# Turning V's weights with VectorE instead of TensorE in a conditioned attention kernel

## The chip, the cores and the metric

The kernel runs on one core of one Trainium2 chip. The metric is the device time of one execution in microseconds. Before the change the median of three runs is 736.79 us (736.71 to 736.79). A core has five engines that run their own instruction streams side by side: TensorE (PE in the profile, its weight loads PEld), VectorE (DVE), ScalarE (ACT), GpSimd (POOL) and SyncE (SP), which here only issues DMA transfers. They wait for each other through semaphores.

## What is computed

The reference is one attention layer over x (8 batches, 512 positions, 512 channels, float32) with a token per batch that conditions queries and keys, and a residual:

```
Q = split_heads(x @ Wq.T + bq);  K, V likewise      # 16 heads of 32
tQ = split_heads(tokens @ Wq.T + bq);  tK likewise  # one token per batch
cQ = Q + tQ;  cK = K + tK
attn = softmax(cQ @ cK.T / sqrt(32))
out  = x + merge_heads(attn @ V)
```

## The kernel before

The work is cut into 32 groups: 8 batches times 4 groups of four heads (128 channels). Channels of a group lie on the 128 partitions. All weight matrices must be turned, because the product contracts over the input channel, so `wT["q"]`, `wT["k"]` and `wT["v"]` hold W transposed: partition = input channel within a block of 128, then four such blocks, then 512 output channels.

The order of the instructions on TensorE, VectorE, ScalarE and GpSimd is written out by hand (`manual_schedule`): each engine takes its instructions in the order of the program text. SP is left to the planner, which places its DMA issues by when their buffers come free. PSUM is one tile of eight banks of 512 floats; `bank(i)` names one, and the table `TURNS` names the banks of each stage by place.

**The head of the program**, up to about 28 us, is where the change lies. The first loads are x's first batch, then the weights in rows of 2 KB: `load_w` (L175 to L178), one DMA of 256 KB per 128 rows, so that partition p of block c holds row c·128+p of W. Behind them on SP's queue stand bvb and bvs (copies of the bias of V) and then, by `load_block`, the blocks of x's second batch, in runs of 128 bytes: `spread` (L135) views a 512x512 matrix so that row f·32+j goes to partition j, place f, and takes 32 columns. Such a block, turned by VectorE in squares of 32x32 (`turn_x`, L310), is x transposed, without TensorE. `load_residual` (L159, L169) loads and biases the x that is added at the end, and writes it out in the same spread layout.

`transpose_w` (L249) turns 128 rows of a weight matrix with four TensorE transposes (L253) into one PSUM bank, from which VectorE (L260, L264) or ScalarE (L262, L266) copies it to `wT`. `project_qk_part` (L337) is one of the four products, one per block of input channels, of a group's queries or keys in the plain form; `project_qk_end` adds the token's part on the way out of PSUM: VectorE for q (L350), ScalarE for k (L352). The first two groups' q and k come from this plain form. All later projections use a form with seven products in place of eight (`first_products`, `other_products`, L390 and L393), whose sums of weight blocks GpSimd makes once (`combine_w`, L282 to L285) from `wT`, into the buffers of the raw weights.

The token's part of q or k is `condition` (L644: four products of the tokens with wT, one per quarter of TensorE's columns, then a ScalarE copy L646) and `condition_end`: four TensorE transposes of that copy (L631), a reduction by VectorE (L653) and an addition of the bias (L659; VectorE for q, GpSimd for k).

In the text the last steps of the head run like this: the last eight of k's weight transposes, w_v's first four, `condition_end("q")`, `condition("k")`, w_v's next four, `condition_end("k")`, w_v's last eight, with q's and k's group 0 finished between, and then all of q's second group in bank 7. After that come `combine_w` and the first row of scores: `row_max(0, 0)` (L486 on TensorE, four score tiles; L477 and L495 on VectorE, their row maxima), `denominators` (L505 on ScalarE, the exponentials with their sums), the second group's k (L337, finished by ScalarE's L352), the second row of scores, and the first seven-product stage for q (L393).

**The body** goes over the groups t, four stages each; a stage holds 4 tiles of exponentials (L547 and L550 on TensorE, L561 on ScalarE), one row of scores of the next group with its maxima and sums, and either one stage of a projection for the next batch or the products of the group before with V (L566). `split_max` (L519 to L522, GpSimd) cuts the row maxima into three bfloat16 parts, which TensorE transposes (L531) and adds to the scores. GpSimd takes its work in program order too, so a biasing of a residual (L169) can stand ahead of a split_max.

Of the kernel before, what the change touches and what calls it, by code (L numbers as in the profile page):

```python
# [17 lines left out]
def kernel(  # L18
# [38 lines left out]
    nc = tc.nc  # L57
    P = 128
# [4 lines left out]
    HG = P // HD  # L63
    NP = HG // 2
    NS = S // P
    NC = D // P
# [65 lines left out]
    BL = 32  # L132
    NB = S // BL

    def spread(a, d):  # L135

        return a.rearrange("(f j) d -> j f d", j=BL)[:, :, d : d + BL]
# [33 lines left out]
    ws = {}  # L171
# [3 lines left out]
    def load_w(n, w, queue, cs=range(NC)):  # L175
        wv = w.rearrange("(c p) d -> p c d", p=P)
        for c in cs:
            queue.dma_start(ws[n][:, c, :], wv[:, c, :])  # L178
# [29 lines left out]
    load_w("k", Wk, nc.sync, [0])  # L208
    load_w("q", Wq, nc.sync, [1, 2, 3])
    load_w("k", Wk, nc.sync, [1, 2, 3])  # L210
    load_w("v", Wv, nc.sync)
    bvb = const.tile([P, D], F32, tag="bvb", name="bvb")
    nc.sync.dma_start(bvb, bv.rearrange("(o d) -> o d", o=1).broadcast_to([P, D]))
    bvs = const.tile([P, G, BL], F32, tag="bvs", name="bvs")
# [18 lines left out]
    for i in range(NS):  # L233
# [11 lines left out]
    wT = {  # L245
        n: const.tile([P, NC, D], F32, tag=f"wT{n}", name=f"wT_{n}") for n in ("q", "k", "v")
    }

    def transpose_w(n, dc, pt, odd=None):  # L249

        odd = dc % 2 if odd is None else odd
        for cc in range(NC):
            nc.tensor.transpose(  # L253
                pt[:, cc * P : (cc + 1) * P], ws[n][:, dc, cc * P : (cc + 1) * P], ident
            )
        o = wT[n][:, :, dc * P : (dc + 1) * P]
        pv = pt.rearrange("p (c s) -> p c s", c=NC)
        if n == "q":
            if odd:
                nc.vector.tensor_scalar(o, pv, SCALE, None, ALU.mult)  # L260
            else:
                nc.scalar.activation(o, pv, AF.Copy, scale=SCALE)  # L262
        elif odd:
            nc.vector.tensor_copy(o, pv)  # L264
        else:
            nc.scalar.copy(o, pv)  # L266
# [62 lines left out]
    def pair_of(t, n):  # L329

        if (n, t // 2) not in pairs:
            pairs[n, t // 2] = qkp.tile([P, 2, S], F32, tag=n, name=f"{n}T_{t // 2}")
        return pairs[n, t // 2]

    def project_qk_part(t, n, cc, pt):
        b, g = divmod(t, G)
        nc.tensor.matmul(  # L337
            pt,
            wT[n][:, cc, g * P : (g + 1) * P],
            xT[b][:, cc, :],  # L340
            start=(cc == 0),
            stop=(cc == NC - 1),
        )

    def project_qk_end(t, n, pt):
        b, g = divmod(t, G)
        o = pair_of(t, n)[:, t % 2, :]
        add = tok[:, "qk".index(n), g, b : b + 1]
        if n == "q":
            nc.vector.tensor_scalar(o, pt, add, None, ALU.add)  # L350
        else:
            nc.scalar.activation(o, pt, AF.Identity, bias=add)  # L352
        qkT[n, t] = o

    def project_qk(t, n, pt):
        for cc in range(NC):
            project_qk_part(t, n, cc, pt)
        project_qk_end(t, n, pt)
# [281 lines left out]
    def condition(n, pt):  # L640


        for cc in range(NC):
            nc.tensor.matmul(pt[cc * HD : (cc + 1) * HD, :], condT[:, cc, :], wT[n][:, cc, :])  # L644
        part[n] = const.tile([P, D], F32, tag=f"part{n}", name=f"part_{n}")
        nc.scalar.copy(part[n], pt)  # L646

    def condition_end(n, pt, on):

        i = "qk".index(n)  # L650
        untranspose(part[n], pt)
        sum4 = const.tile([P, NC, B], F32, tag=f"sum4{n}", name=f"sum4_{n}")
        nc.vector.tensor_reduce(  # L653
            sum4,
            pt.rearrange("p (d c e) -> p d e c", d=NC, c=NC)[:, :, 0:B, :],
            AX.X,
            ALU.add,
        )
        on.tensor_tensor(  # L659
            tok[:, i], sum4, bias2[:, i, :].unsqueeze(2).broadcast_to([P, NC, B]), ALU.add  # L660
        )
# [5 lines left out]
    def bank(i):  # L667
        return psum[:, i, :]
# [27 lines left out]
    condition("q", bank(6))  # L696
    transpose_w("k", 2, bank(3), 1)
    transpose_w("k", 3, bank(7), 0)
    transpose_w("v", 0, bank(0), 1)
    condition_end("q", bank(1), nc.vector)  # L700
    project_qk_end(0, "q", pq)
    condition("k", bank(5))
    transpose_w("v", 1, bank(6), 1)
    condition_end("k", bank(0), nc.gpsimd)
    transpose_w("v", 2, bank(3), 0)
    project_qk_end(0, "k", pk)
    transpose_w("v", 3, bank(1), 1)
    project_qk(1, "q", bank(7))
    for n in ("q", "k", "v"):
        combine_w(n)  # L710

# [266 lines left out]
```

## Time and profile before

| what | value |
|---|---|
| median of three runs | 736.79 us |
| the profiled execution: its time | 736.38 us |
| its span, first to last instruction | 734.3 us |
| mean granted TensorE clock in it | 0.999 of full speed |
| TensorE busy | 726.8 us, 99% of the span |
| ScalarE busy | 618.9 us, 84% |
| VectorE busy | 530.0 us, 72% |
| GpSimd busy | 182.8 us, 25% |
| w_v's four DMA issues on SP | from 8.3 to 9.7 us, each landed 4.8 to 5.5 us later |
| w_v's sixteen transposes on TensorE | 19.4 to 23.4 us |

The difference of 2.1 us between the profiled execution's time and its span is what lies before the first and after the last instruction. In the rows of the profile, the first number is the start in us from the beginning of the span, the second the duration; a merged row with "x8" gives the duration of all eight. A float32 product shows as two passes, so four products read x8 in the L337 and L644 rows, while transposes read one each. In brackets stands how long the engine had been idle and what ended that.

### The profile page before, as it was taken

The numbers are of one execution on the slowest core, as the hardware profiler recorded it, in microseconds if no ns is written. First come the engines' busy times: TensorE is split into PE (matmuls) and PEld (weight loads), VectorE is DVE, ScalarE is ACT, GpSimd is POOL, SyncE is SP. The second block draws the span as 40 slices with busy tenths as digits, with TensorE's granted clock in tenths as the row PEclk, the third lists the DMA queues.
The fourth block names the chain that finished last, engine by engine and source line by source line (L and its number), as shares of the span: only waits on it lengthen the run. The fifth ranks groups of instructions, "written<-read, shape, count | busy, mean of one in ns | idle before, by whom it ended". The sixth has DMA issues, their size and how long they took to land.

```text
span 734.3 us, 15120 instructions
## 1 busy us (share of the span) xinstructions
PE 726.8 (99%) x5432; PEld 405.7 (55%) x5432; DVE 530.0 (72%) x844; ACT 618.9 (84%) x1543; POOL 182.8 (25%) x282
## 2 busy tenths in 40 slices
PE   9999999999999999999999999999999999999997
PEld 6566555665555565555565555565555566555422
DVE  3688776776777876777776877777767777767665
ACT  2478988988988988988989888988988899898665
POOL 3720211222211122221122221122221122221363
PEclk9999999999999999999999999999999999999999
DMA  8521212222212212211212221212110111110112
GB/s 260 88 45 29 45 23 36 40 34 45 44 28 32 44 30 44 45 31 29 44 30 44 44 34 25 44 30 44 29 24 10 28 30 29 30 27 10 24 16 43
DMA packets 194270, 29.63 MB, mean 40 GB/s; under 512 B 190986, under 2 KB 192010, under 8 KB 194196
## 3 DMA queue, kind: packets, MB, share of 16 engines
q1 hardware_dynamic: 193616, 28.01, 22.9%
q8 instruction: 42, 0.69, 0.4%
q10 hardware_dynamic: 580, 0.68, 0.3%
q14 instruction: 32, 0.26, 0.1%
HBM read 20.27 MB, written 8.39 MB: 39 GB/s over the span
## 4 chain that ended last, share of the span: by engine, by line
PE 97%; ACT 1%; DVE 1%; DMA 1%; issue 0%; POOL 0%; DVEq 0%; POOLq 0%
PE psum L393 26%; PE psum L566 16%; PE psum L486 15%; PE psum L550 15%; PE psum L390 14%; PE psum L547 6%; PE psum L337 2%; PE psum L531 1%; PE psum L253 1%; ACT e L561 1%; DMA x<-in_x_dram 1%; PE psum L576 0%; PE psum L298 0%; DVE nmax L495 0%; PE psum L644 0%; PE psum L631 0%
## 5 line engine op out<-in xcount | busy, mean ns | idle before, releaser
L505 ACT ACTIVATE dead<-psum,nmax 128x512 f32<-128x512 f32 x480 | 327.0, 701 | 7.8 <-DVE nmax L477 5.4
L561 ACT ACTIVATE e<-psum 128x512 f32<-128x512 f32 x512 | 264.4, 603 | 77.9 <-PE psum L550 77.8
L477 DVE TENSOR_REDUCE nmax<-psum 128x1 f32<-128x512 f32 x240 | 154.6, 686 | 144.4 <-PE psum L486 144.4
L495 DVE TENSOR_REDUCE nmax<-psum 128x2 f32<-128x1024 f32 x136 | 164.7, 1216 | 10.4 <-PE psum L486 9.1
L623 POOL TENSOR_TENSOR res<-res,recs 128x512 f32<-128x512 f32 x31 | 33.3, 1076 | 446.8 <-DVE res L622 446.8
L486 PE MATMUL psum<-kT,qT 32*128 32x512 f32 x1024 | 136.3, 601 | 0.0
L550 PE MATMUL psum<-qT,kT 32*128 32x512 f32 x1024 | 133.0, 589 | 0.0
L566 PE MATMUL psum<-e,v 128*32 128x512 f32 x1024 | 120.5, 597 | 0.0
L505 ACT ACTIVATION_READ_ACCUMULATOR dead<-psum,nmax 128x1 f32 x480 | 104.9, 218 | 0.0
L486 PEld LDWEIGHTS psum<-kT,qT 32*128 32x128 f32 x1024 | 57.7, 183 | 56.6 <-ACT dead L505 19.7
L566 PEld LDWEIGHTS psum<-e,v 128*32 128x32 f32 x1024 | 26.3, 110 | 65.2 <-issue 37.7
L547 PE MATMUL psum<-maxT,onesb 3*128 3x512 bf16 x512 | 52.6, 385 | 0.0
L550 PEld LDWEIGHTS psum<-qT,kT 32*128 32x128 f32 x1024 | 51.1, 186 | 2.4 <-issue 0.2
L390 PE MATMUL psum<-wc_v,xc 128*128 128x256 f32 x192 | 49.5, 380 | 0.4 <-ACT e L561 0.4
L547 PEld LDWEIGHTS <-onesb 3*128 3x128 bf16 x512 | 13.5, 91 | 61.5 <-issue 51.8
L393 PE MATMUL psum<-xc,wc_q 128*128 128x256 f32 x180 | 46.2, 379 | 0.0
L393 PE MATMUL psum<-xc,wc_k 128*128 128x256 f32 x180 | 46.2, 379 | 0.0
L624 POOL TENSOR_TENSOR res<-res,xr 128x512 f32<-128x512 f32 x31 | 40.4, 1302 | 2.4
L169 POOL TENSOR_TENSOR xr<-xr,bvs 128x512 f32<-128x512 f32 x31 | 39.3, 1268 | 3.2 <-DMA xr<-in_x_dram 2.9
L390 PEld LDWEIGHTS psum<-wc_v,xc 128*128 128x128 f32 x192 | 36.4, 190 | 6.1 <-ACT e L561 1.3
L390 PE MATMUL psum<-wT_v,xT 128*128 128x256 f32 x128 | 38.8, 405 | 0.0
L393 PEld LDWEIGHTS psum<-xc,wc_q 128*128 128x128 f32 x180 | 34.3, 190 | 4.6
(156 smaller groups left out, 778.5 us busy)
## 6 DMA issues: line engine op xcount, KB each, us to landing
xr<-in_x_dram SPq DMA_DIRECT2D x124, 64.0 KB, 2.5
out_dram<-res SPq DMA_DIRECT2D x124, 64.0 KB, 2.0
x<-in_x_dram SPq DMA_DIRECT2D x112, 64.0 KB, 2.3
w_q<-in_L_cond_Wq_dram SPq DMA_DIRECT2D x4, 256.0 KB, 4.5
w_k<-in_L_cond_Wk_dram SPq DMA_DIRECT2D x4, 256.0 KB, 4.3
w_v<-in_L_cond_Wv_dram SPq DMA_DIRECT2D x4, 256.0 KB, 5.2
x<-in_x_dram ACTq DMA_DIRECT2D x2, 256.0 KB, 4.4
x<-in_x_dram SPq DMA_DIRECT2D x2, 256.0 KB
```

What stands on the lines that cost most here:

```text
L169: nc.gpsimd.tensor_tensor(xr[t], xr[t], bias, ALU.add)
L390: nc.tensor.matmul(pt, xb, w, start=(kc == kcs[0]), stop=(kc == kcs[-1]))
L393: nc.tensor.matmul(pt, w, xb, start=(kc == kcs[0]), stop=(kc == kcs[-1]))
L477: nc.vector.tensor_reduce(nmax[t][:, qc, j : j + 1, 0], banks(HG + j), AX.X, ALU.max, negate=True)
L486: nc.tensor.matmul(pt, qkT["q", t][r, qc * P : (qc + 1) * P], qkT["k", t][r, :], start=True, stop=True,)
L495: nc.vector.tensor_reduce(nmax[t][:, qc, pr * 2 : pr * 2 + 2, 0], pt, AX.X, ALU.max, negate=True)
L505: nc.scalar.activation(dead, banks(HG + j), AF.Exp, bias=nmax[t][:, qc, j, :], accum_out=sums[t][:, qc, j, :],)
L547: nc.tensor.matmul(bank[j], onesb[r, :], maxT[t][r, :], start=True, stop=False)
L550: nc.tensor.matmul(bank[j], qkT["k", t][r, kc * P : (kc + 1) * P], qkT["q", t][r, :], start=False, stop=True,)
L561: nc.scalar.activation(e[:, i, :], bank[pr * 2 + i], AF.Exp)
L566: nc.tensor.matmul(pt[j * HD : (j + 1) * HD, :], vs[b % 2][:, kc, (g * HG + j) * HD : (g * HG + j + 1) * HD], es[t, kc, j // 2][:, j % 2, ...
L624: nc.gpsimd.tensor_tensor(y, y, xr.pop(t), ALU.add)
```

## The change

V's weights are loaded in sixteen DMAs of 64 KB instead of four of 256 KB, in runs of 128 bytes (32 floats) instead of 2 KB, in the layout that `spread` makes: partition h·32+j of block cc holds, for f from 0 to 15, the 32 columns from cc·128+h·32 of row f·32+j. The four calls of `transpose_w("v", ...)` go: sixteen transposes on TensorE, three copies on VectorE, one on ScalarE. Four VectorE transposes of 128x512 take their place, after `project_qk_end(0, "k")` in the text, which on VectorE puts them behind the reduction of `condition_end("k")` and ahead of the end of q's second group. Two of the four products of q's second group (bank 7) move up between `condition("k")` and `condition_end("k")`; the other two stay after it.

```
-    load_w("v", Wv, nc.sync)
+    wv = ws["v"].rearrange("p c (f e) -> p c f e", e=BL)
+    for cc in range(NC):
+        for h in range(HG):
+            nc.sync.dma_start(
+                wv[h * BL : (h + 1) * BL, cc], spread(Wv, cc * P + h * BL)
+            )
...
     transpose_w("k", 3, bank(7), 0)
-    transpose_w("v", 0, bank(0), 1)
     condition_end("q", bank(1), nc.vector)
     project_qk_end(0, "q", pq)
     condition("k", bank(5))
-    transpose_w("v", 1, bank(6), 1)
+    for cc in range(2):
+        project_qk_part(1, "q", cc, bank(7))
     condition_end("k", bank(0), nc.gpsimd)
-    transpose_w("v", 2, bank(3), 0)
     project_qk_end(0, "k", pk)
-    transpose_w("v", 3, bank(1), 1)
-    project_qk(1, "q", bank(7))
+    for cc in range(NC):
+        nc.vector.transpose(wT["v"][:, cc, :], ws["v"][:, cc, :])
+    for cc in range(2, NC):
+        project_qk_part(1, "q", cc, bank(7))
+    project_qk_end(1, "q", bank(7))
```

In the built program SP's order changes too: the blocks x_8 and x_9 of the third batch's x are issued ahead of the residual load xr_0, x_10 ahead of xr_1, x_11 ahead of xr_2; before, xr_0, xr_1 and xr_2 went first.

## The prediction

> **What bounds the kernel now.** I read the page's busy shares first, then the chain that ended last.
>
> ```profile
> PE 726.8 (99%) x5432; PEld 405.7 (55%) x5432; DVE 530.0 (72%) x844; ACT 618.9 (84%) x1543; POOL 182.8 (25%) x282
> PE 97%; ACT 1%; DVE 1%; DMA 1%; issue 0%; POOL 0%; DVEq 0%; POOLq 0%
> ```
>
> TensorE is busy 99% of the span and carries 97% of the chain. So work taken from TensorE shortens the run, as long as nothing else is late where the gap closes. The change lies between 8 and 60 us, so I read the timeline there.
>
> ```profile
> 18.47 1.09 PE L253 MATMUL psum<-ident,w_k 128*128 128x128 f32 x8
> ...
> 19.40 0.60 PE L253 MATMUL psum<-ident,w_v 128*128 128x128 f32 x4
> ...
> 19.61 0.59 ACT L266 COPY wT_k<-psum 128x512 f32<-128x512 f32 x1 [0.41 <-PE psum L253]
> ...
> 20.37 0.16 PEld L644 LDWEIGHTS psum<-wT_k,condT 128*32 128x32 f32 x8 [0.17 <-ACT wT_k L266]
> 20.37 1.06 PE L644 MATMUL psum<-wT_k,condT 128*32 128x512 f32 x8
> ...
> 21.37 0.66 PE L253 MATMUL psum<-ident,w_v 128*128 128x128 f32 x4
> 21.50 0.58 ACT L646 COPY part_k<-psum 128x512 f32<-128x512 f32 x1 [1.31 <-PE psum L644]
> ...
> 22.14 0.66 PE L631 MATMUL psum<-ident,part_k 128*128 128x128 f32 x4
> 22.64 1.04 PE L253 MATMUL psum<-ident,w_v 128*128 128x128 f32 x8
> 22.84 0.29 DVE L653 TENSOR_REDUCE sum_k<-psum 128x32 f32<-128x128 f32 x1
> ...
> 23.51 3.60 PE L337 MATMUL psum<-xT,wT_q 128*128 128x512 f32 x8
> ```
>
> A row is start, duration, engine, line. The w_v rows go away; the L337 row is q's second group, of which half moves up. Next, what follows:
>
> ```profile
> 27.22 0.75 DVE L350 TENSOR_SCALAR qT<-psum,tok 128x512 f32<-128x512 f32 x1 [2.82 <-PE psum L337]
> 28.20 1.29 DVE L477 TENSOR_REDUCE nmax<-psum 128x1 f32<-128x512 f32 x2 [0.23 <-PE psum L486]
> 28.92 0.69 ACT L505 ACTIVATE dead<-psum,nmax 128x512 f32<-128x512 f32 x1 [4.48 <-DVE nmax L477]
> 31.74 1.14 PE L486 MATMUL psum<-kT,qT 32*128 32x512 f32 x8
> 32.05 0.69 ACT L352 ACTIVATE kT<-psum,tok 128x512 f32<-128x512 f32 x1
> 32.81 0.92 PE L393 MATMUL psum<-xT,wT_q 128*128 128x256 f32 x3
> ```
>
> This chain decides the forecast. ScalarE's second kT (L352) ends at 32.05+0.69 = 32.74 and TensorE's L393 starts at 32.81. It must wait: its first product goes to bank 4, which that kT reads (both take place 1 of their row of TURNS, 4 in each). The list of waits agrees:
>
> ```profile
> PEld psum L393 <- ACT kT L352: 0.8, 1, 0.8
> ```
>
> So VectorE and ScalarE have next to no slack at 32.8, though neither is the bound of the kernel.
>
> **TensorE alone.** Sixteen transposes go. The first four (19.40 to 19.84) are worth nothing: the token's product for k starts at 20.37, released by ScalarE's copy of wT_k that ends at 20.20, and that copy waits for k's own transposes, which don't move. Without w_v, TensorE idles there. The next four end a stretch of 22.14-21.37 = 0.77, of which 0.44 is work and the rest the wait for part_k (ready at 22.08). The last eight are 23.51-22.64 = 0.87. Together 1.64.
> In their place, q's first half starts at 21.37 plus 0.06 (eight transposes behind L644 took 0.93, elsewhere 0.87), lasts four passes of 0.43 = 1.72, and ends at 23.15, so part_k is no longer waited for. Its four transposes take 0.43, to 23.58; the second half, with the 0.09 that L337 spends in front of L486 (27.04-23.51 is 3.53, eight passes are 3.44), ends at 25.40. Before, L486 started at 27.04: 1.64 earlier.
>
> **kT of group 0, now later against TensorE.** part_k's transposes start at 23.15 (before: 22.14). VectorE's sum_k follows 0.64 to 0.70 later (23.08 to 23.71 for the last w_v copy, 22.14 to 22.84 here): 23.79 to 23.85, end at most 24.14. GpSimd's tok: 0.08 of wait and 0.24. ScalarE then starts 0.05 to 0.30 later (no row shows it waiting for GpSimd; before, its kT stood at 23.75 behind another copy, 0.30 after tok ended at 23.45), and takes 0.69: 25.1 to 25.45. Against 25.40 that is at most 0.1 of wait, covered by what comes next.
>
> **VectorE: three copies go, four transposes of w_v come, and where they stand is the price.** Program order puts them between sum_k and q's second L350. VectorE is idle from 22.0 (the end of q's first L350) to sum_k, so an earlier place would be free; this one isn't. Nearest row: the transpose of x, the same 128x512 f32 from SBUF to SBUF.
>
> ```profile
> 45.17 0.70 DVE L310 STREAM_TRANSPOSE xT<-x 128x512 f32<-128x512 f32 x1
> 45.26 2.50 POOL L169 TENSOR_TENSOR xr<-xr,bvs 128x512 f32<-128x512 f32 x2
> ```
>
> Two in a row take 1.29 and the second starts 0.62 after the first. From sum_k (23.82) it goes: 0.25 to the first transpose, 4 x 0.62 = 2.48, L350 0.67 start to start: L477 starts at 27.22. By TensorE it could have started at 25.40+1.16 = 26.56 (28.20-27.04 = 1.16). Before it was 28.20, so this chain gains 0.98, not 1.64. ScalarE follows L477 step for step, so its second kT ends at 32.74-0.98 = 31.76, and L393 starts at about 31.83, while TensorE would be there at 31.17. It idles for about 0.65 and keeps a gain of 0.98. Bounds by the spread of these steps (pace 0.60 to 0.65, first step 0.23 to 0.32, sum_k 23.79 to 23.85): 0.8 to 1.1. If the chain had slack I don't see, 1.64.
> GpSimd's wc_q runs beside the transposes. Row first: above, a transpose beside a GpSimd operation takes 0.70, the four of x 0.67 to 0.70, and the two GpSimd operations 1.25 each, their usual time. The Trainium skill, SBUF — State Buffer, § Summary: rules for kernel authors, says that when VectorE runs in a two-port mode the one of the two that issues second blocks fully until the other ends. By it each transpose could wait for one 1.26 us operation, 5 us in all and a slower kernel; by the row, nothing. I take the row.
> Behind L393 the order repeats every 4.29 us with TensorE back to back, so all else shifts along.
>
> **w_v's loads.** 4 issues of 256 KB become 16 of 64 KB in 128-byte runs, on SP's queue ahead of bvb, bvs and x's blocks. Nearest row:
>
> ```profile
> 14.14 9.69 SPq L145 DMA_DIRECT2D x<-in_x_dram  x16
> ```
>
> That is 0.61 per issue; the xr ones take 6.32/12 = 0.53. From 8.26, sixteen are issued by 16.7 to 18.0 and landed 2.5 later, 20.5 at the latest. By bytes: 1.05 MB at the 109 to 133 GB/s of 18 to 30 us, behind 3.15 MB of x, w_q and w_k (moved by about 11.0, adding up GB/s by stretch), is 7.9 to 9.6: at most 20.6[...]. VectorE wants them at 24.07: hidden.
> The rule against this: DMA: Bandwidth & Descriptors, § Measured, gives 0.95 us for 64 KB and calls smaller transfers descriptor-dominated. Sixteen in series are 15.2 (estimate): 26.2, some 28 landed, and about 3.8 us on VectorE's chain: 739.6. By the rows, 735.8. I take the rows: same runs, same queue.
> SP's queue behind it is some 7.5 us later: x_4 goes out at about 21.6, the fourth block lands at 34, wanted at 43.5. The build also puts the residual loads xr_0 and xr_1 behind the blocks x_8 and x_9, x_10, which wait for VectorE's transposes at 50 and 56 us. xr_1 then lands at about 61 (before: by 33), and GpSimd's addition to it stands in front of split_max of group 1 (65.11 before, about 64 now), whose result TensorE uses at 70.12 before, 69 now. 1.27+1.23 after 61 is 63.5: hidden, with 5 us to spare.
>
> **The sum.** The profiled execution has a span of 734.3 and a time of 736.38; minus 0.98 that is 733.3 and 735.4. The median of the runs is 736.79, 0.41 above: 735.8.
>
> **Rivals.** I call a change within 0.2% (1.47 us) the same: that is about what a measurement of this kernel can tell from no change.
> Full gain: ScalarE's kT isn't what holds L393, and all of 1.64 stays: 735.15. For it: no idle time is shown before L393 now. Against it: 32.74 to 32.81, and the list of waits.
> No gain: VectorE's chain is 1 us longer than I make it (0.25 more per transpose, or kT of group 0 late by 1.7): 736.8. Against: a TensorE idle from 20 to 22 on VectorE leaves only known rows.
> Slower: w_v lands late. From 24.07 on each us is one us on L350 and so on L393; at 25.05 the gain is gone, at 26.5 the kernel is 0.2% slower; with the page's figure it lands at 28: 739.6. For it: DMA engines are full up to 16 us and now carry eight thousand small packets after that. Against: x's blocks kept 109 to 133 GB/s in just this form.
>
> **How the numbers follow.** VectorE's chain 0.60 (735.6 to 736.0, with run scatter 735.4 to 736.2), full gain 0.18, no gain 0.12, late w_v 0.10. Faster: 0.18 and the edge of the first, 0.20. Slower 0.10. Same 0.70. Range: down past full gain with 0.15 of scatter, 735.0; up to no gain, 736.8.
>
> **What would show it.** Right: L486 of group 0 at about 25.4; VectorE's four transposes back to back at about 24.1 with L350 at 26.5 behind them; TensorE idle about 0.65 in front of the first product of q at about 31.8, released by ScalarE's kT; TensorE idle some 0.5 in front of the token's product for k at 20.37. Wrong: first product at 31.2 (full gain), transposes over 0.8 each, or w_v's last landing after 24.

## The result, and the profile after

The changed kernel takes 734.68 us (median of eight runs, 734.44 to 734.89); the kernel before, beside it on the same chip, 736.69 (736.3 to 737.04). The ratio is 0.9973 (95% interval 0.9964 to 0.9982): 2.0 us faster, where 1.0 was forecast and the range ended at 735.0. The profiled execution took 734.58 us with a span of 732.6 (before: 736.38 and 734.3), at the same granted clock, 0.999.

In the changed kernel the line numbers of the body are 6 higher: L399 is the L393 of before, L492 is L486, L483 is L477, L358 is L352, L356 is L350, L343 is L337, L637 is L631, L650 is L644, L659 is L653; L713 holds the new transposes.

The page's busy shares and chain, and its group of w_v's loads (KB each, median us from issue to landing):

```profile
PE 725.0 (99%) x5416; PEld 402.8 (55%) x5416; DVE 530.4 (72%) x845; ACT 619.1 (85%) x1542; POOL 183.2 (25%) x282
...
PE 97%; ACT 1%; DMA 1%; DVE 1%; issue 0%; SPq 0%; POOL 0%; DVEq 0%; POOLq 0%
...
w_v<-in_L_cond_Wv_dram SPq DMA_DIRECT2D x16, 64.0 KB, 3.3
```

TensorE has lost its sixteen instructions and 1.8 us, and is the bound as before. The timeline of the head, the same stretch that the prediction read:

```profile
18.38 1.09 PE L259 MATMUL psum<-ident,w_k 128*128 128x128 f32 x8
...
19.31 0.60 PE L637 MATMUL psum<-ident,part_q 128*128 128x128 f32 x4
19.51 0.59 ACT L272 COPY wT_k<-psum 128x512 f32<-128x512 f32 x1 [0.41 <-PE psum L259]
...
20.15 1.07 PE L650 MATMUL psum<-wT_k,condT 128*32 128x512 f32 x8 [0.24 <-ACT wT_k L272]
...
21.15 1.98 PE L343 MATMUL psum<-xT,wT_q 128*128 128x512 f32 x4
...
22.97 0.60 PE L637 MATMUL psum<-ident,part_k 128*128 128x128 f32 x4
...
23.41 1.88 PE L343 MATMUL psum<-xT,wT_q 128*128 128x512 f32 x4
23.68 0.29 DVE L659 TENSOR_REDUCE sum_k<-psum 128x32 f32<-128x128 f32 x1 [2.43 <-PE psum L637]
...
23.89 2.49 DVE L713 STREAM_TRANSPOSE wT_v<-w_v 128x512 f32<-128x512 f32 x4
...
24.25 1.28 POOL L288 TENSOR_TENSOR wc_q<-wT_q 128x512 f32<-128x512 f32 x1
...
25.22 1.14 PE L492 MATMUL psum<-kT,qT 32*128 32x512 f32 x8
25.61 1.27 POOL L289 TENSOR_TENSOR wc_q<-wc_q,wT_q 128x512 f32<-128x512 f32 x1
...
26.30 0.71 DVE L356 TENSOR_SCALAR qT<-psum,tok 128x512 f32<-128x512 f32 x1
...
26.93 1.27 DVE L483 TENSOR_REDUCE nmax<-psum 128x1 f32<-128x512 f32 x2
...
27.64 0.69 ACT L511 ACTIVATE dead<-psum,nmax 128x512 f32<-128x512 f32 x1 [2.62 <-DVE nmax L483]
...
29.92 1.14 PE L492 MATMUL psum<-kT,qT 32*128 32x512 f32 x8
...
30.77 0.69 ACT L358 ACTIVATE kT<-psum,tok 128x512 f32<-128x512 f32 x1
...
31.51 1.13 PE L399 MATMUL psum<-xT,wT_q 128*128 128x256 f32 x4 [0.45 <-ACT kT L358]
```

Nearly every step that the prediction worked out for the head can be read off here. L483 on VectorE has no bracket, so it follows L356 directly: VectorE's order holds it, not the scores that L492 had begun at 25.22. TensorE's idle 0.45 in front of L399 ends with ScalarE's kT; the list of waits says the same of it:

```profile
PE psum L399 <- ACT kT L358: 0.4, 1, 0.4
```

The start of the program varies from one execution to the next by up to 1.2 us (17.3 to 18.5 for the product named here, in all the traces of this study): the token's product for q (L650, before L644) begins at 17.48 in the trace of before and at 17.39 here. So from here on places in the head are counted from the start of that product. L399 stands 14.12 behind it (31.51 - 17.39); before, L393 stood at 15.33 (32.81 - 17.48). **The head gained 1.21.**

The way from L399 to the first exponential of the body is the same in both (17.56), and the body from the first to the last exponential took 674.73 before, and 674.94 and 674.72 in two executions of the changed kernel: no gain there. But from the last exponential to the end of the span it is 9.17 before and 8.55 after. **The end gained 0.62**, in a part of the program that the change doesn't touch. In sum -1.21 at the head, -0.62 at the end, +0.21 in the body and -0.09 at the start: -1.71, and the spans differ by 1.70.

The end of the program in the timeline, of before:

```profile
728.73 0.26 DVE L925 RECIPROCAL rec<-psum 128x16 f32<-128x16 f32 x1 [0.25 <-PE psum L631]
729.53 0.76 DVE L936 TENSOR_TENSOR res<-psum,rec 128x256 f32<-128x256 f32 x2 [0.54 <-PE psum L933]
...
730.78 0.40 SPq L944 DMA_DIRECT2D out_dram<-res  x1
```

and of the changed kernel, which does the same work:

```profile
722.72 0.72 DVE L628 STREAM_TRANSPOSE res<-psum 128x512 f32<-128x512 f32 x1 [0.29 <-issue]
...
727.65 0.26 DVE L933 RECIPROCAL rec<-psum 128x16 f32<-128x16 f32 x1 [0.25 <-PE psum L637]
728.10 0.76 DVE L944 TENSOR_TENSOR res<-psum,rec 128x256 f32<-128x256 f32 x2 [0.19 <-DVE rec L933]
...
729.35 0.40 SPq L952 DMA_DIRECT2D out_dram<-res  x1
```

Two places differ. Behind the last reciprocal VectorE pauses 0.54 before and 0.19 after: -0.35. And from SyncE's last issue of an output DMA to the end of the span it is 3.48 before (734.26 - 730.78) and 3.22 after (732.57 - 729.35): -0.26, with the same transfer.

### The profile page after: what moved, and what is told of

It reads as the page before. It is cut to its first block, busy times and chain, and to the rows that moved or that the text cites. A ratio compares the mean times of both kernels' runs of the same rounds, so it can differ in the third digit from the quotient of the medians.

```text
span 732.6 us, 15105 instructions
## 1 busy us (share of the span) xinstructions
PE 725.0 (99%) x5416; PEld 402.8 (55%) x5416; DVE 530.4 (72%) x845; ACT 619.1 (85%) x1542; POOL 183.2 (25%) x282
## 4 chain that ended last, share of the span: by engine, by line
PE 97%; ACT 1%; DMA 1%; DVE 1%; issue 0%; SPq 0%; POOL 0%; DVEq 0%; POOLq 0%
PE psum L399 26%; PE psum L572 16%; PE psum L492 15%; PE psum L556 15%; PE psum L396 14%; PE psum L553 6%; PE psum L343 2%; PE psum L537 1%; DMA w_k<-in_L_cond_Wk_dram 1%; ACT e L567 1%; PE psum L259 0%; PE psum L582 0%; DVE nmax L501 0%; PE psum L650 0%; PE psum L603 0%
## 5 line engine op out<-in xcount | busy, mean ns | idle before, releaser
L483 DVE TENSOR_REDUCE nmax<-psum 128x1 f32<-128x512 f32 x240 | 154.6, 686 | 143.7 <-PE psum L492 143.7
L492 PE MATMUL psum<-kT,qT 32*128 32x512 f32 x1024 | 136.4, 601 | 0.0
L492 PEld LDWEIGHTS psum<-kT,qT 32*128 32x128 f32 x1024 | 57.7, 183 | 56.8 <-ACT dead L511 22.2
L399 PE MATMUL psum<-xc,wc_k 128*128 128x256 f32 x180 | 46.2, 379 | 0.0
L399 PE MATMUL psum<-xc,wc_q 128*128 128x256 f32 x180 | 46.2, 379 | 0.0
L399 PEld LDWEIGHTS psum<-xc,wc_k 128*128 128x128 f32 x180 | 34.2, 190 | 4.6
```

Of the source, the lines that this page charges most:

```text
L399: nc.tensor.matmul(pt, w, xb, start=(kc == kcs[0]), stop=(kc == kcs[-1]))
L483: nc.vector.tensor_reduce(nmax[t][:, qc, j : j + 1, 0], banks(HG + j), AX.X, ALU.max, negate=True)
L492: nc.tensor.matmul(pt, qkT["q", t][r, qc * P : (qc + 1) * P], qkT["k", t][r, :], start=True, stop=True,)
```

## The experiments

The theories at the outset. **Head:** TensorE has 1.6 us less to do, but the chain over VectorE's transposes, L356, L483 and ScalarE's kT allows a gain of 1.2 only; the rival says that TensorE's own work, and not this chain, sets the gain. **End:** something that depends on the program's instructions or DMAs and not on their time; the rival says that the 0.62 is scatter between executions.

### The kernel before, once more (b_again)

The kernel is unchanged.

> The kernel before once more, unchanged, for a second trace. The changed kernel's span is 1.70 shorter: 1.30 at the first exponential of group 0 (50 us), 1.08 at the last one, then 0.62 more behind the last TensorE work (0.35 where VectorE's first result of the last group waits, 0.27 in SP's waits for the last DMAs). If the 0.62 is a property of the program, the end looks here as in the first trace of the kernel before: VectorE's L936 starts 0.54 behind its reciprocal, and SP passes six semaphore waits after the last landing. If it is scatter between executions, the end differs here by some tenths. The body's drift (0.22) should be scatter, and so be of another size here.

737.02 us; the kernel before beside it 736.4. The span is 0.6 longer than in the first trace, and all of it lies at the start (the token's product for q begins at 18.11). Everything behind that repeats to 0.02: L393 at 15.33, the body 674.71, VectorE's pause 0.54, the end 9.17. So the end is a property of the program and not scatter; the start is scatter.

### The changed kernel, once more (a_again)

> The changed kernel, unchanged, on the chip of the following two, for comparison: 734.7 (2.0 below the kernel before), its end as in its first trace.

734.56 us (734.21 to 734.9) against 736.4: 0.9973 (0.9962 to 0.9984). L399 at 14.12 with 0.45 of idle time before it, the end 8.55 with a pause of 0.19: all as in the first trace. The gain is 1.84 by these medians, 2.0 by the first; 1.83 is what head and end make together, and the difference is scatter between runs.

### Before, with w_v loaded in eight DMAs (b_lanes)

Still 2 KB rows of W, but each DMA split into two halves of 256 columns (1 KB runs): four DMAs more, no other instruction changed.

```
-    load_w("v", Wv, nc.sync)
+    wvv = Wv.rearrange("(c p) d -> p c d", p=P)
+    for c in range(NC):
+        for hf in range(2):
+            hs = slice(hf * HS, (hf + 1) * HS)
+            nc.sync.dma_start(ws["v"][:, c, hs], wvv[:, c, hs])
```

> The kernel before with w_v loaded in 8 DMAs of 128 KB (half rows of 1 KB) instead of 4 of 256 KB, all else the same. DMAs take one of eight completion semaphores in turn, so four more DMAs move every later DMA by four places, as the changed kernel's twelve more do. Theory of the semaphores' turn: the end is shortened as in the changed kernel, by 0.3 (SP's waits alone) to 0.6, and nothing changes at the head: 736.1 to 736.4, with the last exponential's start unmoved. Rival, that the shorter end is scatter or comes with the earlier head: the same as the kernel before, 736.7.

735.86 us against 736.4: 0.9991 (0.9982 to 1.0). The head hasn't moved (L393 at 15.34). VectorE's pause is still there, and the stretch behind SyncE's last issue has the length that it has in the changed kernel; the end of the timeline:

```profile
729.53 0.76 DVE L940 TENSOR_TENSOR res<-psum,rec 128x256 f32<-128x256 f32 x2 [0.54 <-PE psum L937]
...
730.78 0.39 SPq L948 DMA_DIRECT2D out_dram<-res  x1
```

733.99 - 730.78 is 3.21 instead of 3.48. The end is 8.89, 0.28 shorter, by four DMAs at the other end of the program. (The medians are 0.54 apart, with an interval from 0 to 1.3 us; the trace accounts for 0.28.) What the trace's records of SyncE show: DMAs signal their end on eight semaphores in turn, and at the end of the program SyncE waits for these in a fixed order, in seven waits. Before, the last DMA to land signals the semaphore of the first wait; six further waits follow it at 0.06 to 0.07 us each. With four DMAs more (or twelve, as in the change; both shift the turn by four) the last DMA signals the semaphore of the fifth wait, and two follow. The four that have passed by then took 0.25 before.

### The changed kernel, with bvs loaded in eight DMAs (a_lanes)

Four DMAs more than the changed kernel: sixteen more than before, which brings the turn back to where it stood before.

```
-        nc.sync.dma_start(
-            bvs[h * BL : (h + 1) * BL],
-            bv.rearrange("(o g h e) -> o h g e", o=1, g=G, h=HG)[:, h].broadcast_to([BL, G, BL]),
-        )
+        for g2 in range(2):
+            gs = slice(g2 * 2, g2 * 2 + 2)
+            nc.sync.dma_start(
+                bvs[h * BL : (h + 1) * BL, gs],
+                bv.rearrange("(o g h e) -> o h g e", o=1, g=G, h=HG)[:, h, gs].broadcast_to([BL, 2, BL]),
+            )
```

> The changed kernel with the small bvs loads in 8 DMAs instead of 4, so that the turn of the eight semaphores is again that of the kernel before (sixteen more DMAs in all). Theory of the semaphores' turn: the head as in the changed kernel (L399 at 31.5), the end as in the kernel before: 0.3 to 0.6 slower than the changed kernel, 735.0 to 735.3. Rival: as the changed kernel, 734.7.

735.23 us against 736.4: 0.9983 (0.9975 to 0.9992), 0.67 slower than the changed kernel in the same set of runs. The head is the changed kernel's (L399 at 14.13, 0.45 of idle time), VectorE's pause is 0.19, and from SyncE's last issue (729.33) to the end (733.17) it is 3.84. The waits at the end stand as before the change, which explains 0.26 of the loss (3.48 against 3.22). Most of the other 0.36 is a pause of SyncE between two of these waits, 0.34 where the kernel before has 0.03. So the time lies in the expected range, but in good part for a reason outside the theory.

The records show where this pause comes from. Counted from 0 in order of start, SyncE's stream stands still for 0.33 us or more in front of its records 79, 207, 335 and 463, which are 128 apart, in every trace of this study that has so many. Here SyncE has 470 records, and 463 is the wait behind the pause. The kernel before has 454 and ends ahead of it. The changed kernel has 466, and its record 463 stands behind the last of the seven waits; from that wait to the end it is 0.76 there and 0.75 in the kernel before, so the pause costs it nothing. No run moves this pause alone.

### Before, with half of q's second group moved up (b_split)

The second part of the change alone; w_v is loaded and turned as before.

```
     transpose_w("v", 1, bank(6), 1)
+    for cc in range(2):
+        project_qk_part(1, "q", cc, bank(7))
     condition_end("k", bank(0), nc.gpsimd)
...
     transpose_w("v", 3, bank(1), 1)
-    project_qk(1, "q", bank(7))
+    for cc in range(2, NC):
+        project_qk_part(1, "q", cc, bank(7))
+    project_qk_end(1, "q", bank(7))
```

> The kernel before with only the split: the first half of q's second group moves up between w_v's second four transposes and part_k's, the rest stays behind w_v's last eight. V's weights are still turned by TensorE. Theory of the chain: only TensorE's wait for part_k (0.33 of the 0.77) is filled; VectorE has no transposes, so L477 follows TensorE at 1.16 and ScalarE's kT keeps its place against L393: everything behind is 0.3 earlier, 736.1 to 736.4 where the kernel before takes 736.4 to 736.7. Rival, that ScalarE's chain holds L393 in any case: no change.

736.11 us against 736.5: 0.9995 (0.9986 to 1.0003). In the trace L486 comes at 9.23 instead of 9.56 and L393 at 15.00 instead of 15.33, without idle time: 0.33, the wait for part_k that the products fill. The end is 9.17.

### The changed kernel without that half (a_nosplit)

The first part of the change alone: all four products of q's second group behind the transposes.

```
     condition("k", bank(5))
-    for cc in range(2):
-        project_qk_part(1, "q", cc, bank(7))
     condition_end("k", bank(0), nc.gpsimd)
...
-    for cc in range(2, NC):
+    for cc in range(NC):
         project_qk_part(1, "q", cc, bank(7))
```

> The changed kernel without the split: all four products of q's second group behind condition_end of k. TensorE then waits from 21.15 to 21.93 for part_k and starts L492 of group 0 at about 25.85 instead of 25.22. Theory of VectorE's chain: its transposes now start at 22.85 and are through before q's second group is; L483 starts at 27.0 instead of 26.93, and the first seven-product stage at 31.6 instead of 31.51: within 0.1 to 0.2 of the changed kernel, 734.7 to 734.8, because what the split gains on TensorE is lost again in the wait before L399. Rival, that TensorE alone counts: 0.63 slower than the changed kernel.

734.74 us against 736.5: 0.9976 (0.9967 to 0.9986). TensorE in the timeline:

```profile
21.95 0.66 PE L637 MATMUL psum<-ident,part_k 128*128 128x128 f32 x4 [0.71 <-ACT part_k L652]
...
31.74 1.13 PE L399 MATMUL psum<-xT,wT_q 128*128 128x256 f32 x4
```

TensorE now waits 0.71 for part_k, and L492 comes at 8.56 instead of 7.83: 0.73 later. Yet L399 comes only 0.21 later (14.33) and without idle time. So of the 0.73 that the moved half saves TensorE, VectorE's chain lets 0.21 through. That speaks against the rival: were TensorE's work the measure, all of it would be seen.

### The transposes where VectorE is idle (a_free)

Two of the four go behind the last turns of q's weights, two behind the end of q's group 0; all are over before sum_k.

```
     transpose_w("q", 3, bank(1), 1)
+    for cc in range(2):
+        nc.vector.transpose(wT["v"][:, cc, :], ws["v"][:, cc, :])
     for cc in range(NC):
         project_qk_part(0, "k", cc, pk)
...
     project_qk_end(0, "q", pq)
+    for cc in range(2, NC):
+        nc.vector.transpose(wT["v"][:, cc, :], ws["v"][:, cc, :])
     condition("k", bank(5))
...
     project_qk_end(0, "k", pk)
-    for cc in range(NC):
-        nc.vector.transpose(wT["v"][:, cc, :], ws["v"][:, cc, :])
```

> The changed kernel with the four transposes where VectorE is idle: two of them behind its copy of q's last weights (from 14.4), two behind q's first group (from 21.2), none behind sum_k. Theory of VectorE's chain: L483 starts 1.16 behind L492, at 26.4, ScalarE's kT ends at 30.95, and TensorE's idle 0.45 before L399 is gone: 0.45 faster than the changed kernel, 734.1 to 734.3. Rival, that the wait before L399 has another cause (ScalarE's exponentials, bank 4): the idle time stays, and the time with it.

734.06 us (733.97 to 734.28) against 736.5: 0.9967 (0.9955 to 0.9979). The timeline:

```profile
26.61 1.29 DVE L483 TENSOR_REDUCE nmax<-psum 128x1 f32<-128x512 f32 x2 [0.23 <-PE psum L492]
...
30.47 0.69 ACT L358 ACTIVATE kT<-psum,tok 128x512 f32<-128x512 f32 x1
...
31.23 1.13 PE L399 MATMUL psum<-xT,wT_q 128*128 128x256 f32 x4
```

L483 waits for TensorE again, as before the change; the idle time before L399 is gone, and L399 stands at 13.61 (31.23 - 17.62), 0.51 earlier, with TensorE's work unchanged. The place of the transposes cost the change that much. Against the kernel before (15.33) the head now gains 1.72, all that L492 gained on TensorE (1.73). The end is 8.55 as in the change.

### Each transpose twice (a_twice)

The same four results, each written twice.

```
-    for cc in range(NC):
+    for cc in [c for c in range(NC) for again in range(2)]:
         nc.vector.transpose(wT["v"][:, cc, :], ws["v"][:, cc, :])
```

> The changed kernel with each of the four transposes done twice (the same result twice), all in the same place. Theory of VectorE's chain: four more at 0.62 put q's second group, L483, kT and L399 off by 2.48 each, and the time by 2.5: 737.1 to 737.3, slower than the kernel before; TensorE idle 2.9 in front of L399. Rival, that VectorE has slack there: 0 to 0.5.

739.91 us (739.58 to 740.73) against 736.5: 1.0048 (1.0036 to 1.0061), 2.6 to 2.8 us more than expected. Up to L399 the chain moves as the theory says, but further: eight transposes take 5.47, and L399 comes 2.99 later than in the changed kernel, where 2.48 was expected. TensorE's idle time, expected as 2.9 in one piece, comes in two, in front of the second row of scores and in front of L399. And the first exponential of the body comes 5.64 later. TensorE and VectorE in the timeline, and then the stretches of 2 us (busy time of PE, PEld, DVE, ACT and POOL, then the granted clock, DMA share and GB/s):

```profile
23.80 5.47 DVE L713 STREAM_TRANSPOSE wT_v<-w_v 128x512 f32<-128x512 f32 x8
...
31.37 1.87 PE L492 MATMUL psum<-kT,qT 32*128 32x512 f32 x8 [1.47 <-ACT dead L511]
...
34.41 2.07 PE L399 MATMUL psum<-xT,wT_q 128*128 128x256 f32 x4 [1.16 <-ACT kT L358]
```

```profile
30.00:32.00 2.00, 0.63 (x2) 0.29 (x2) 2.00 (x3) 1.45 (x4) 1.92 (x3) 1.00 0.59 91
32.00:34.00 2.00, 1.24 (x8) 0.30 (x6) 1.67 (x4) 1.67 (x5) 2.00 (x2) 0.75 0.00 0
34.00:36.00 2.00, 1.59 (x4) 1.33 (x5) 1.07 (x1) 0.35 (x1) 1.92 (x3) 0.50 0.00 0
36.00:38.00 2.00, 2.00 (x7) 1.55 (x6) 0.00 (x0) 1.48 (x4) 2.00 (x2) 0.50 0.00 0
38.00:40.00 2.00, 2.00 (x7) 1.58 (x5) 0.76 (x2) 1.58 (x6) 1.28 (x2) 0.55 0.00 0
```

The granted clock falls from 1.00 to 0.50 at about 33.0 us (the stretch from 32 has a mean of 0.75) and is back at about 39.8 (0.55 from 38 to 40): 6.8 us. The first four passes of L399 take 2.07 instead of 1.13. That is the other 2.65 (5.64 - 2.99). The first idle time, 1.47, ends at 31.37, 1.6 ahead of the fall. The second, 1.16, begins at 33.25, when the clock has already fallen; it can't have brought the fall on, and whether it made it longer was not tried. The Trainium skill, TensorE: Matmul & The Clock Gate, Part 1, lets the clock fall to half after an idle window of about 3.4 us, counted by a window that runs on its own; here no single idle time was half that long. So the page's length is no safe bound here; that the idle time is the cause is argued from its place, not shown by a run of its own.

### Two transposes more (a_six)

The first two results written twice.

```
-    for cc in range(NC):
+    for cc in (0, 0, 1, 1, 2, 3):
         nc.vector.transpose(wT["v"][:, cc, :], ws["v"][:, cc, :])
```

> The changed kernel with two of the four transposes done twice, six in all behind sum_k. With eight, L399 came 2.9 later (0.67 per transpose) and the granted clock then read 0.50 from 34 to 38 us, which made 2.65 more. Theory of VectorE's chain: two more cost 2 x 0.67 = 1.34, TensorE idles 1.4 to 1.8 before L399 in one piece or nearly so, and the clock stays at 1.00: 735.9 to 736.1. Theory that a wait of over 1 us costs clock: 1.34 and 1 to 2.6 more, 737 to 738.6.

736.64 us (736.57 to 738.33) against 736.51: 1.0006 (0.9997 to 1.0015), where 735.9 to 736.1 was expected. In the trace L399 comes 1.50 later (expected 1.34), behind one idle time of 1.23, at a granted clock of 1.00. The end is 8.55. Three of its eleven runs lie at 737.1 to 738.3; no trace shows what they had. The body takes 675.52, 0.6 to 0.8 more. A comparison of VectorE's records with the changed kernel's finds pauses of 0.3 to 0.4 in other places than there: two records more in VectorE's stream have shifted them, and behind two of the new places, at 331.7 and 406.6 us, the later steps stay some 0.3 later each. That these two make the 0.6 is read from this one trace. The next experiment tests such a pause by itself.

### Before, with eight more instructions on VectorE at the start (b_dve8)

The theory: VectorE's sequencer pauses at fixed places of its stream, whatever stands there. In the kernel before, record 1215 (counted from 0 in order of start, waits for semaphores included) lies between the last reciprocal and the first product behind it, on the chain that ends last; the changed kernel's stream has eight records more, and the pause falls in front of a transpose that has time: the `[0.29 <-issue]` above. So eight more records of any kind should do it:

```
-    nc.vector.memset(which, 0.0)
+    for _ in range(9):
+        nc.vector.memset(which, 0.0)
```

> The kernel before with eight more small memsets of the same tile by VectorE at the start (16 numbers each, in VectorE's idle time before 5.8 us), nothing else. In the four traces with the kernel before's VectorE stream the last group's first result starts 0.54 behind the reciprocal, in the six with the changed kernel's (eight records more) 0.19. Theory that VectorE's sequencer pauses at a fixed place of its stream, which eight more records move into an idle stretch: 0.19 here, and 0.35 faster than the kernel before. Rival, that the pause belongs to TensorE's transposes of w_v or to the DMAs: 0.54, the same time.

736.1 us against 736.51: 0.9993 (0.9984 to 1.0002), 0.41 less, with an interval that reaches past 1. The timeline shows where it went:

```profile
723.88 0.72 DVE L623 STREAM_TRANSPOSE res<-psum 128x512 f32<-128x512 f32 x1 [0.28 <-issue]
...
728.83 0.26 DVE L926 RECIPROCAL rec<-psum 128x16 f32<-128x16 f32 x1 [0.25 <-PE psum L632]
729.27 0.75 DVE L937 TENSOR_TENSOR res<-psum,rec 128x256 f32<-128x256 f32 x2 [0.19 <-DVE rec L926]
```

The pause has moved to the place that it has in the changed kernel, and the end is 8.81: 0.36 less. From SyncE's last issue (730.52) to the end (734.0) it is 3.48, as before: the DMAs were left alone. The two effects at the end are separate, and b_lanes and b_dve8 each show one: 0.28 + 0.36 = 0.64, against the 0.62 of the change.

In the traces of all runs together, such pauses of about 0.4 stand in front of VectorE's records 191, 319, 575, 703, 831 and 1215: places that lie 128 or a multiple of it apart, like SyncE's. At the others of that series (63, 447, 959 and 1087) VectorE is mostly still at work, and none can be told apart. Of the six traces that the expectation counts, five have the changed kernel's number of records; a_twice has twelve more than the kernel before.

### A further move of q's second group (a_best, a_best2)

On top of a_free, one of the two early products goes ahead of the token's product for k, where TensorE is idle:

```
     project_qk_end(0, "q", pq)
     for cc in range(2, NC):
         nc.vector.transpose(wT["v"][:, cc, :], ws["v"][:, cc, :])
+    project_qk_part(1, "q", 0, bank(7))
     condition("k", bank(5))
-    for cc in range(2):
-        project_qk_part(1, "q", cc, bank(7))
+    project_qk_part(1, "q", 1, bank(7))
```

> The transposes where VectorE is idle, as in the run that put them there, and q's second group cut otherwise: its first product stands ahead of the token's product for k (in TensorE's idle time there), the second behind it, the last two behind part_k's transposes. Theory of the head: with VectorE's chain out of the way TensorE is the bound, so its last idle time in the head counts in full: L492 0.4 to 0.45 earlier than with the first half behind the token's product, ScalarE's kT still in time (0.05 before the first seven-product stage), 0.4 faster than that run: 733.6 to 733.8. Rival: group 0's kT (sum_k, GpSimd, ScalarE: 2.25 from part_k's transposes to L492) becomes the wait; then 0.1 to 0.2 faster.

734.22 us against 736.51: 0.9969 (0.9956 to 0.9981): nothing gained on a_free. TensorE's timeline shows why:

```profile
20.29 1.13 PE L343 MATMUL psum<-xT,wT_q 128*128 128x512 f32 x2 [0.24 <-ACT wT_k L272]
```

The product writes bank 7, where k's last weights lie until ScalarE has copied them, so it waits for the same copy as the token's product did, and L399 comes 0.19 later than in a_free. In a_best2 k's last weights go to bank 0:

```
-    transpose_w("k", 3, bank(7), 0)
+    transpose_w("k", 3, bank(0), 0)
```

> As the run with the first product of q's second group ahead of the token's product for k, with k's last four transposes in bank 0 instead of bank 7. In that run TensorE waited 0.24 before the product, released by ScalarE's copy of k's weights out of bank 7, into which the product writes; that pushed everything behind it back. Theory that bank 7 was the cause: the product starts behind part_q's transposes without a wait, L492 comes 0.4 earlier than in that run and 0.2 earlier than with the first half behind the token's product (7.63 behind the token's product for q, where that one has 7.83 and the changed kernel 7.83): 733.8 to 734.0, the fastest of all by 0.1 to 0.2. Rival, that the product waits for ScalarE's copy for another reason: 734.2 again.

734.07 us (733.87 to 735.01) against 736.32: 0.9971 (0.996 to 0.9982). The wait is gone and L399 stands at 13.30, 0.31 earlier than in a_free (L492 at 7.53, where 7.63 was expected). The times don't tell the two apart. Either is some 2.3 to 2.4 us below the kernel before and, by the traces, 0.5 to 0.8 ahead of the change at L399.

## Why the prediction was wrong

The direction of each step was right and the head's mechanism held; the forecast failed mainly by what was taken as zero, the end of the program.

**The step that failed** is "Behind L393 the order repeats ..., so all else shifts along", and with it the sum, which took nothing but 0.98 from the profiled time. The body did shift along. The end did not: it became 0.62 shorter, by 0.28 of SyncE's waits (b_lanes) and 0.35 of VectorE's pause (b_dve8). Head alone, 736.69 - 1.21 = 735.5, lies within 0.2% of the time before and within the range; the 0.62 took it out of both. The head's 0.23 above the forecast had a part in it: with 0.98 and 0.62 the time would have been 735.09, just inside the range. The prediction doesn't take up the end at all: the `[0.54 <-PE psum L933]` in front of the last products stood in the trace of before, though nothing in that trace says that it would go.

**TensorE alone, 1.64.** Nearly right. L492 of group 0 came 1.73 earlier (7.83 against 9.56); 25.4 was forecast, 25.31 at the start of before. The first four transposes of w_v, called worth nothing, were worth 0.13: the token's product for k begins 0.05 after ScalarE's copy instead of 0.17, as 2.76 against 2.89 shows, once TensorE is there before it. The idle time in front of it was there, 0.40 from where part_q's transposes left off (19.31 + 0.44) to 20.15, where some 0.5 was named.

**kT of group 0** was on time. L492 at 25.22 stands behind it with no idle time.

**VectorE's chain, 0.98 kept of 1.64.** The mechanism was right, step for step: transposes between sum_k and L356, L483 right behind, ScalarE's kT, TensorE idle in front of L399, released by that kT. a_free (wait gone, 0.51 back), a_nosplit (0.73 on TensorE, 0.21 at L399) and a_twice (2.99 at L399, and as much from sum_k's end to L356) show it three ways. The size was off: 1.21 against 0.98, and above the bound of 1.1. Each step was a little shorter than taken: sum_k 0.05 earlier, 0.21 instead of 0.25 to the first transpose, 2.41 instead of 2.48 for the four, 0.63 instead of 0.67 from L356 to L483, 0.03 behind that. The idle time was 0.45, not 0.65.

**GpSimd beside the transposes.** The row was right to be taken: the transposes took 0.67 to 0.71 and GpSimd's operations beside them 1.28 and 1.27. The blocking that the Trainium skill, SBUF — State Buffer, § Summary: rules for kernel authors, states for two-port modes isn't seen here; whether these transposes run in such a mode no run shows.

**w_v's loads** were hidden. Sixteen issues lie between 8.2 and 19.1, 0.68 each on the mean: twelve steps of 0.48 to 0.58, as in the rows, and three of 1.0 to 1.6. That is below the 0.95 for 64 KB of the Trainium skill, DMA: Bandwidth & Descriptors, § Measured, a figure for DMAs that GpSimd issues to 128 partitions; these are issued by SyncE, to 32. The last of them landed at 20.93 (20.5 or 20.6 was forecast), wanted at 23.89. x_4's first issue came at 21.66 (21.6 was forecast), and the fourth block landed at 31.8, where 34 was forecast.

**The residuals** behind x_8 to x_10 were hidden too: GpSimd biased the second at 60.71, and split_max of group 1 stood at 63.82, where about 64 was forecast.

**The rivals.** Full gain came nearest by its time (735.15), for the wrong reason: 1.64 is not what the head gave. Neither no gain nor late loads has a trace for it.

## What to carry to other kernels

Where the gain is some tenths of a per cent, the end of the program belongs to the working: what stands between the last exponential and the end of the span can change by 0.6 us through the mere number of instructions and DMAs ahead of it, and one run with idle instructions added, or a load split, tells that part from the change itself. Work moved from the bounding engine to another is priced by the place it gets on that other: the same four transposes cost 0.5 us between two links of a chain, and nothing where that engine was idle.

## What the runs showed of the hardware

- VectorE's stream pauses for about 0.4 us at fixed records, multiples of 128 apart (191, 319, 575, 703, 831 and 1215). On the chain that ends last, this is 0.36 us that eight idle instructions take away (0.54 to 0.19 behind the reciprocal).
- SyncE's stream pauses for 0.33 us or more at its records 79, 207, 335 and 463; in a_lanes the last of these adds some 0.3 us to the end.
- SyncE's waits at the end cost 0.28 us more or less, by the number of DMAs in the program: six waits or two follow the last landing.
- An idle time of TensorE of 1.47 us, 1.6 us ahead, and one of 1.16 us within it, went with a fall of the granted clock from 1.00 to 0.50 for 6.8 us, and 2.65 us of time. One of 1.23 (a_six) and one of 0.45 (the change) left it at 1.00 in their profiles.
